# Layer 1's convolution and layer 2's embedding as parts of layer 2's table of slots

## The chip, the core and the metric

One core of a Trainium2 chip runs the whole program. Its engines take their instructions in order, each from its own queue: PE (TensorE, matrix products into PSUM), DVE (VectorE), ACT (ScalarE), POOL (GpSimd, which also issues the indirect gathers) and SP (which issues most DMAs). The metric is the device time of one execution in microseconds; ten runs of the kernel before give the median. All data are 32-bit floats.

## The reference, cut to what matters

Four images of 128 channels, 48x48, pass through a state-space layer (layer 0), a deformable convolution (layer 1), eight performer blocks (layer 2), a mixture of experts, causal attention (layer 3) and a second mixture. The change touches layers 1 and 2.

```python
# layer 1: deformable 3x3 convolution, batch norm, relu
off_out = conv3x3(x, w_off) + b_off             # 27 channels: dy, dx, mask for 9 taps
py, px = gy + ky + dy, gx + kx + dx             # where each tap samples
sampled = bilinear(x, py, px) * sigmoid(mask)   # 4 corners, zero outside
out = relu(scale * einsum('oik,bikhw->bohw', weight, sampled) + shift)
# layer 2, t = tokens of out: [4, 2304, 128]
h = layernorm(t) @ tok_W + tok_b + pe           # the embedding
for i in range(8):                              # performer
    h = h + attn(layer_norm(h), i)              # key features are summed over all tokens of an image
    h = h + gelu(layer_norm(h) @ W1[i] + b1[i]) @ W2[i] + b2[i]
    if i == 3: h = gelu(h @ enc + enc_b) @ dec + dec_b
t = t + tanh(h)
```

## The kernel before

An image has 2304 tokens: 18 tiles of 128 tokens, or 6 blocks of 384 (`BLK`, three tiles, `G3`). Four images make 24 blocks (`NBL`). The state of the tokens is one SBUF tile `T` (`h` in layer 2) of 128 partitions x 72 tiles x 128 channels.

**Layer 1 (`_layer1`, L878 to L970)** comes first and alone. For an image it loads the 27 offset channels (L908), works out positions, table rows and four corner weights per tap on DVE (L911 to L939, the mask's sigmoid on ACT at L934), and then goes through the 18 tiles. A tile has nine taps. For each tap POOL gathers 128 rows of 4x128 values from a table in DRAM that layer 0 wrote (L949; a row holds the four corners; eight buffers `g`), DVE multiplies by the four corner weights into another buffer `gw` (L956), and PE turns and sums the four corners at once as four ordinary products with the identity (L962), three taps to a PSUM tile `pt`. ACT copies `pt` to `sT` (L965). Then nine products with the convolution's weights and one with the shift (L968, L969) and a relu on ACT (L970) give the tile of `T`. The order is left to a scheduler.

**The embedding (L1108 to L1129)** follows, image by image: `T` is stored to DRAM as `kept` (L1115), its statistics are measured on DVE (`measure`, L1078 and L1079), `finish` raises the variance to -1/2 on POOL (L1086), the normed block (L1093) is turned on PE, copied, multiplied by `tok_w` (L1126), and added to the position table `pe` (L1127, which holds `tok_b` too since L1110).

**Layer 2's table of slots.** Its eight layers have 8 x 24 = 192 blocks, and a loop over slots writes the order of PE, ACT, DVE and POOL out by hand; SP's order alone is the scheduler's. In slot s the block s gets its keys and values (`k1`, `k2`, `k3`; `k0` of block s+1 norms on POOL and adds a bias to `h` on POOL, L1165), the block s-9 its queries (`q0` to `q2`; `LAG` = 9), the block before that its attention output (`q3` to `q6`), and the block s-12 its feed-forward part (`f0` to `f4`; `FLAG` = 12). `rotated` adds two halves of a rotary embedding on POOL (L1180). After an image's last keys, pieces put aside (`some`) sum its key features (L1301, L1311). So slots 0 to 8 have key work alone, slots 9 to 11 have queries too, and from slot 12 on all three.

Of the kernel before, what the change touches and what calls it, by code (L numbers as in the profile page):

```python
# [15 lines left out]
F32 = mybir.dt.float32  # L16
# [7 lines left out]
P = 128  # L24
NB = 4
# [845 lines left out]
def layer1(env, io, table, offs, T):  # L871


    with ExitStack() as ctx:
        _layer1(ctx, env, io, table, offs, T)


def _layer1(ctx, env, io, table, offs, T):  # L878
    nc, tc, ident = env.nc, env.tc, env.ident
    cp = ctx.enter_context(tc.tile_pool(name="l1c", bufs=1))  # L880
    sp = ctx.enter_context(tc.tile_pool(name="l1s", bufs=2))
    ps = ctx.enter_context(tc.tile_pool(name="l1p", bufs=3, space=PSUM))
    po = ctx.enter_context(tc.tile_pool(name="l1o", bufs=2, space=PSUM))
# [3 lines left out]
    w = cp.tile([P, TAPS, C], F32, name="w")  # L887
    nc.sync.dma_start(w, io["l1_w"])


    def row(name):
        t = cp.tile([P, C], F32, name=name)
        nc.scalar.dma_start(t, io[name].to_broadcast([P, C]))
        return t

    scale, shift, mean, var = (row("l1_" + n) for n in ("gamma", "beta", "mean", "var"))
    nc.vector.tensor_scalar_add(var, var, 1e-5)
    nc.scalar.sqrt(var, var)
    nc.vector.reciprocal(var, var)
    nc.vector.tensor_mul(scale, scale, var)  # L900
    nc.vector.tensor_mul(mean, mean, scale)
    nc.vector.tensor_sub(shift, shift, mean)
    for t in range(TAPS):
        nc.vector.tensor_mul(w[:, t, :], w[:, t, :], scale)

    for b in range(NB):
# [35 lines left out]
        for i in range(NT):  # L942
            sT = sp.tile([P, TAPS, P], F32, name="sT")
            for t0 in range(0, TAPS, 3):
                pt = ps.tile([P, 3, P], F32, name="pt")
                for t in range(t0, t0 + 3):
                    g = sp.tile([P, 4 * C], F32, name="g", bufs=8)
                    j = i * TAPS + t
                    nc.gpsimd.indirect_dma_start(  # L949
                        out=g,  # L950
                        out_offset=None,
                        in_=table,
                        in_offset=bass.IndirectOffsetOnAxis(ap=idx[:, j : j + 1], axis=0),
                    )
                    gw = sp.tile([P, 4, C], F32, name="gw", bufs=4)
                    nc.vector.tensor_mul(  # L956
                        gw,
                        g.rearrange("p (q c) -> p q c", c=C),
                        wq[:, i, t, :].unsqueeze(2).to_broadcast([P, 4, C]),
                    )  # L960
                    for q in range(4):
                        nc.tensor.matmul(  # L962
                            pt[:, t - t0, :], gw[:, q, :], ident, start=q == 0, stop=q == 3
                        )
                nc.scalar.copy(sT[:, t0 : t0 + 3, :], pt)  # L965
            out = po.tile([P, C], F32, name="out")
            for t in range(TAPS):
                nc.tensor.matmul(out, sT[:, t, :], w[:, t, :], start=t == 0, stop=False)  # L968
            nc.tensor.matmul(out, env.ones_row, shift[:1, :], start=False, stop=True)  # L969
            nc.scalar.activation(T[:, b * NT + i, :], out, AF.Relu)  # L970
# [25 lines left out]
def layer2(env, io, T):  # L996


    with ExitStack() as ctx:
        _layer2(ctx, env, io, T)  # L1000
# [5 lines left out]
FLAG = LAG + 3  # L1006

# [6 lines left out]
def _layer2(ctx, env, io, T):  # L1014
# [33 lines left out]
    tok_b = cp.tile([P, 1, C], F32, name="tok_b")  # L1048
# [25 lines left out]
    def measure(st, b, j):  # L1074
        mv, rstd = st
        s6 = sp.tile([P, G3, nc.vector.BN_STATS_DIM], F32, name="s6", bufs=3)
        for g in range(G3):
            nc.vector.bn_stats(out=s6[:, g, :], in_=h[:, b * NT + j * G3 + g, :])  # L1078
            nc.vector.bn_aggr(out=mv[:, j * G3 + g, :], in_=s6[:, g, :])  # L1079
# [8 lines left out]
    def normed(st, b, j, engine, name):  # L1088
        mv, rstd = st
        xn = sp.tile([P, G3, C], F32, name=name, bufs=1)  # L1090
        for g in range(G3):
            i = j * G3 + g
            engine.tensor_scalar(  # L1093
                xn[:, g, :],
                h[:, b * NT + i, :],
                mv[:, i, 0:1],
                rstd[:, i : i + 1],
                op0=ALU.subtract,
                op1=ALU.mult,
            )  # L1100
        return xn
# [5 lines left out]

    pe = bp.tile([P, NT, C], F32, name="dk")  # L1108
    nc.scalar.dma_start(pe, io["l2_pe"])
    nc.gpsimd.tensor_add(pe, pe, tok_b.to_broadcast([P, NT, C]))  # L1110
    st1 = []
    for b in range(NB):
        first = stats()
        for j in range(NBLK):
            nc.sync.dma_start(kept[:, at(b, j), :], h[:, at(b, j), :])  # L1115
            measure(first, b, j)
        finish(first, 0, NT)
        st1.append(stats())
        for j in range(NBLK):
            pt = psum(P, BLK)  # L1120
            transposed(normed(first, b, j, nc.vector, "fn"), pt)
            xT = sp.tile([P, BLK], F32, name="uT", bufs=1)
            nc.scalar.copy(xT, pt)
            pp = psum(P, G3, C)
            for g in range(G3):
                nc.tensor.matmul(pp[:, g, :], xT[:, bass.ts(g, P)], tok_w, start=True, stop=True)  # L1126
            nc.vector.tensor_add(h[:, at(b, j), :], pp, pe[:, j * G3 : (j + 1) * G3, :])  # L1127
            measure(st1[b], b, j)
        finish(st1[b], 0, NT)  # L1129
# [32 lines left out]

    def biased(w, r, b, j):
        hb = h[:, at(b, j), :]
        nc.gpsimd.tensor_add(hb, hb, w["bias"][:, r : r + 1, :].to_broadcast([P, G3, C]))  # L1165

    def rotated(w, name, b0, b1, xT, j):

        a = bass.ts(j, BLK)
        pa, pb = psum(P, BLK), psum(P, BLK)  # L1170
        nc.tensor.matmul(pa, w[name], xT, start=True, stop=True)  # L1171
        nc.tensor.matmul(pb, w[name + "r"], xT, start=True, stop=True)  # L1172
        q = sp.tile([P, BLK], F32, name=name, bufs=1)
        r = sp.tile([P, BLK], F32, name="r")
        sq = sp.tile([P, BLK], F32, name=name + "sq", bufs=1)
        nc.vector.scalar_tensor_tensor(q, pa, b0, cos[:, a], op0=ALU.add, op1=ALU.mult)

        nc.scalar.activation(sq, pa, AF.Square, bias=b0)
        nc.vector.scalar_tensor_tensor(r, pb, b1, sin[:, a], op0=ALU.add, op1=ALU.mult)
        nc.gpsimd.tensor_add(q, q, r)  # L1180
        return q, sq
# [19 lines left out]
    def k0(y, n):  # L1201
        t, s, b, j = block(y, n)
        t["xn"] = normed(y.first[b], b, j, nc.gpsimd, "kn")
        biased(y.w, 0, b, j)

    def k1(y, n):
# [10 lines left out]
        t["xT"] = sp.tile([P, BLK], F32, name="xT", bufs=LAG + 2)  # L1217
# [45 lines left out]
    def largest_keys(s):  # L1263
# [7 lines left out]
        def tokens():  # L1271
# [4 lines left out]
            s["xb"] = sp.tile([P, P], F32, name="xb")  # L1276
# [225 lines left out]
    with tc.manual_schedule(engines=ORDERED):  # L1502
        for slot in range(-1, NL * NBL + FLAG + 3):
            i, n = divmod(slot, NBL)
            if i + 1 < NL and n == FLAG + 4:
                layers[i + 1] = Layer(i + 1, layers[i].after)
            if i + 1 < NL and n == NBL - 3:
                prepare(layers[i + 1].w)
            do(q0, slot - LAG)
            do(f1, slot - FLAG)  # L1510
            do(m0, slot - FLAG - 2)
            do(k1, slot)
            some(1)
            do(q3, slot - LAG - 1)
            do(f3, slot - FLAG - 1)
            do(k2, slot)
            do(f2, slot - FLAG)
            do(m1, slot - FLAG - 2)
            some(1)
            do(q1, slot - LAG)  # L1520
            do(k0, slot + 1)
            do(q4, slot - LAG - 1)
            some(1)
            do(k3, slot)
            do(whole, slot)
            do(f0, slot - FLAG + 1)
            do(q5, slot - LAG - 1)
            some(1)
            do(q2, slot - LAG)
            some(1)  # L1530
            do(m2, slot - FLAG - 2)
            do(q6, slot - LAG - 1)
            do(f4, slot - FLAG - 1)
            do(m3, slot - FLAG - 2)

# [656 lines left out]
def program(tc, io, out):  # L2192
    with ExitStack() as ctx:
        env = Env(ctx, tc)
        nc = tc.nc
        with ExitStack() as conv:
            dr = conv.enter_context(tc.tile_pool(name="dr", bufs=1, space=DRAM))
            table = dr.tile([NB * TROWS, 4 * C], F32, name="table")
            offs = dr.tile([P, NB * NT, NOFF], F32, name="offs")
            layer0(env, dr, io, table, offs)  # L2200
            state = ctx.enter_context(tc.tile_pool(name="state", bufs=1))
            T = state.tile([P, NB * NT, C], F32, name="T")
            layer1(env, io, table, offs, T)
        layer2(env, io, T)
# [140 lines left out]
```

## Time and profile before

| what | us |
|---|---|
| median of 10 runs (lowest, highest) | 12663.49 (12636.17, 12673.59) |
| the profiled execution's own time | 12670.15 |
| its span | 12668.0 |
| layer 1's first gather (L949) starts | 5415.3 |
| layer 1's last gather starts | 6318.2 |
| first key copy of layer 2's slot 0 (L1218) starts | 6454.5 |

Times in the profile count from the start of the span. Layer 0 fills the time up to about 5400, layer 2's slots that from 6454 to about 10716, and the rest belongs to the mixtures and layer 3. In rows of groups, the numbers behind the bar are the group's busy time, the mean of one in ns, and the idle time of the engine in front of them with what ended it. PE's records count two per product of 32-bit floats, and one per turn in transpose mode; matmuls are pipelined, so the busy time of a group is less than count times mean. In tables by window the columns are busy us and number of records of each engine, the granted clock of PE as a share of full speed, the busy share of the DMA engines, and GB/s.

### The profile page before, as it was taken

The numbers are of one execution on the slowest core, as the hardware profiler recorded it, in microseconds if no ns is written. First come the engines' busy times: TensorE is split into PE (matmuls) and PEld (weight loads), VectorE is DVE, ScalarE is ACT, GpSimd is POOL, SyncE is SP. The second block draws the span as 40 slices with busy tenths as digits, with TensorE's granted clock in tenths as the row PEclk, the third lists the DMA queues.
The fourth block names the chain that finished last, engine by engine and source line by source line (L and its number), as shares of the span: only waits on it lengthen the run. The fifth ranks groups of instructions, "written<-read, shape, count | busy, mean of one in ns | idle before, by whom it ended". The sixth has DMA issues, their size and how long they took to land.

```text
span 12668.0 us, 192717 instructions
## 1 busy us (share of the span) xinstructions
PE 10962.5 (87%) x71150; PEld 8366.5 (66%) x71150; DVE 8504.5 (67%) x15484; ACT 6888.1 (54%) x13189; POOL 4428.9 (35%) x4775
## 2 busy tenths in 40 slices
PE   6878778877887787689879999999999997799997
PEld 4667666766676666478857777877777776433333
DVE  3998889888888889555456566566565655344444
ACT  3777767777777777411135556555565555232222
POOL 1443333333333334277733333333333332000001
PEclk9999999999999999799979999999999998799998
DMA  2221222122212222266600000000000001200003
GB/s 104 67 70 65 77 79 69 65 75 83 68 65 74 84 65 67 66 180 195 194 13 2 4 4 3 4 2 4 3 3 4 1 1 43 84 6 6 8 8 125
DMA packets 307846, 677.50 MB, mean 53 GB/s; under 512 B 39108, under 2 KB 128984, under 8 KB 304864
## 3 DMA queue, kind: packets, MB, share of 16 engines
q1 hardware_dynamic: 254032, 493.49, 11.8%
q0 software_dynamic: 51840, 169.91, 4.6%
q8 instruction: 571, 9.36, 0.3%
q14 instruction: 363, 2.97, 0.1%
q10 hardware_dynamic: 1040, 1.77, 0.0%
HBM read 602.63 MB, written 71.85 MB: 53 GB/s over the span
## 4 chain that ended last, share of the span: by engine, by line
PE 39%; DVE 6%; ACT 3%; POOL 2%; issue 2%; DMA 2%; SPq 0%; DVEq 0%; ACTq 0%; POOLq 0%
PE psum L1425 4%; PE psum L1417 4%; PE pc L1311 3%; PE psum L1361 3%; PE scT L2061 3%; PE sc L2007 3%; PE out L2090 3%; PE psum L1331 2%; PE psum L1171 2%; POOL g L949 2%; PE psum L1172 2%; DMA g<-table,idx 2%; PE psum L1105 2%; PE psum L1249 1%; PE psum L1350 1%
## 5 line engine op out<-in xcount | busy, mean ns | idle before, releaser
L565 ACT ACTIVATE hs<-ps,bct 128x256 f32<-128x256 f32 x4608 | 1853.4, 474 | 1174.6 <-PE ps L559 1123.0
L559 PE MATMUL ps<-ident,h 128*128 128x128 f32 x9216 | 1489.4, 293 | 781.4 <-DVE h L545 609.2
L559 PEld LDWEIGHTS ps<-ident,h 128*128 128x128 f32 x9216 | 1077.2, 148 | 1166.1 <-DVE h L545 716.3
L573 PE MATMUL yp<-ident,hs 128*128 128x128 f32 x9216 | 1404.7, 288 | 28.4 <-ACT ys L588 28.4
L505 ACT ACTIVATE dA<-delta,l_Al 128x768 f32<-128x768 f32 x1536 | 1388.2, 936 | 0.3
L512 POOL TENSOR_TENSOR h<-du,rB 128x512 f32<-128x512 f32 x768 | 1077.2, 1403 | 766.2 <-PE ps L559 690.4
L573 PEld LDWEIGHTS yp<-ident,hs 128*128 128x128 f32 x9216 | 1156.9, 150 | 84.0 <-ACT ys L588 57.6
L545 DVE TENSOR_TENSOR_SCAN h<-dA,h 128x256 f32<-128x256 f32 (+1 forms) x1024 | 1084.8, 1059 | 27.2
L545 DVE TENSOR_TENSOR_SCAN h<-dA,carry,h 128x768 f32<-128x768 f32 x512 | 1024.1, 2000 | 10.6 <-ACT dA L505 10.6
L1165 POOL TENSOR_TENSOR T<-T,bias 128x384 f32<-128x384 f32 x384 | 383.7, 999 | 1560.4 <-DVE fn L1093 1520.2
L487 POOL TENSOR_SCALAR_AFFINE_SELECT dB<-bct 128x512 f32<-128x512 f32 x768 | 743.6, 968 | 385.6 <-PE b L519 246.8
L2069 ACT ACTIVATE pT<-scT 128x768 f32<-128x768 f32 (+2 forms) x504 | 377.6, 749 | 894.3 <-PE scT L2061 894.0
L519 PE MATMUL b<-dB,duT 128*128 128x128 f32 x6144 | 828.5, 279 | 0.8 <-ACT duT L445 0.8
L545 DVE TENSOR_TENSOR_SCAN h<-dA,carry,b 128x512 f32<-128x512 f32 x512 | 646.1, 1262 | 269.5 <-PE b L519 249.8
L949 POOL DMA_INDIRECT g<-table,idx x648 | 703.5, 1086 | 264.0 <-issue 151.0
L519 PEld LDWEIGHTS b<-dB,duT 128*128 128x128 f32 x6144 | 769.0, 197 | 2.4 <-POOL h L512 1.2
L962 PE MATMUL pt<-ident,gw 128*128 128x128 f32 x5184 | 661.4, 283 | 96.8 <-DVE gw L956 93.4
L956 DVE TENSOR_TENSOR gw<-g,wq 128x512 f32<-128x512 f32 x648 | 446.1, 693 | 421.0 <-DMA g<-table,idx 351.8
L552 POOL COPY carry<-h 128x2 f32<-128x2 f32 x512 | 97.3, 190 | 1781.5 <-DVE h L545 1723.7
L962 PEld LDWEIGHTS pt<-ident,gw 128*128 128x128 f32 x5184 | 608.7, 193 | 144.4 <-DVE gw L956 111.1
L2017 DVE TENSOR_REDUCE mx<-sc 128x2 f32<-128x1024 f32 (+3 forms) x400 | 428.4, 1071 | 363.9 <-PE sc L2007 358.8
L516 DVE TENSOR_TENSOR h<-du,rB 128x512 f32<-128x512 f32 x768 | 632.3, 823 | 3.5 <-DMA rB<-rows 3.5
(345 smaller groups left out, 22968.2 us busy)
## 6 DMA issues: line engine op xcount, KB each, us to landing
rB<-rows SPq DMA_DIRECT2D x768, 384.0 KB, 3.4
w<-f_w SPq DMA_DIRECT2D x64, 1024.0 KB, 12.2
table<-y SPq DMA_DIRECT2D x9, 2304.0 KB, 17.6
table<-tok SPq DMA_DIRECT2D x16, 1152.0 KB, 10.1
g<-table,idx POOLq DMA_INDIRECT x648, 3.7
xb<-x SPq DMA_DIRECT2D x48, 192.0 KB, 2.8
xn<-xn SPq DMA_DIRECT2D x48, 192.0 KB, 3.4
yd<-y SPq DMA_DIRECT2D x4, 2304.0 KB
```

Of the source, the lines that this page charges most:

```text
L487: nc.gpsimd.affine_select(out=x.dB[n], in_=x.bc[:, m0 : m0 + CT // P, n : n + 1].to_broadcast([P, CT // P, P]), pattern=[[0, CT // P], [1, ...
L505: nc.scalar.activation(dA, x.delta[:, d, :], AF.Exp, scale=A[:, d, x.k, n : n + 1])
L512: nc.gpsimd.tensor_mul(h[:, 1, own], x.du[:, 1, own], x.rB[n][:, own])
L516: nc.vector.tensor_mul(x.h[n][:, :, own], x.du[:, :, own], b)
L519: nc.tensor.matmul(b0[:, bass.ts(m, P)], x.duT[:, m, :], x.dB[n][:, m, :], start=True, stop=True,)
L545: nc.vector.tensor_tensor_scan(h, da, b, initial=first, op0=ALU.mult, op1=ALU.add)
L559: nc.tensor.transpose(tt[:, m, bass.ts(d, P)], x.h[n][:, d, bass.ts(2 * q + m, P)], ident)
L565: nc.scalar.activation(hs, tt[:, m, :], AF.Copy, scale=x.bc[:, 2 * q + m, NS + n : NS + n + 1])
L573: nc.tensor.matmul(yp[:, q, (2 * d + m) * P : (2 * d + m + 1) * P], hs[:, bass.ts(d, P)], ident, is_transpose=True, start=n == 0 and m == ...
L949: nc.gpsimd.indirect_dma_start(out=g, out_offset=None, in_=table, in_offset=bass.IndirectOffsetOnAxis(ap=idx[:, j : j + 1], axis=0),)
L962: nc.tensor.matmul(pt[:, t - t0, :], gw[:, q, :], ident, start=q == 0, stop=q == 3)
L1417: nc.tensor.matmul(pg, y.w["w1"][:, bass.ts(f, P)], t["uT"], start=True, stop=True)
```

## The change: positions in front, the convolution three slots ahead, the embedding two

- **Positions.** A new function `positions_of` does L908 to L939 for all four images and stores table rows and corner weights to two DRAM tensors, `index` and `corners`. Each block later loads its own part (27 columns of rows, 27x4 weights) through SP.
- **The convolution** of block n is written into slot n-3. Its steps are nine turns (three taps each), three outputs, and `done` (store to `kept`, statistics, POOL's power). The loop begins three slots earlier. In a turn DVE multiplies in place, for the first of three taps it also adds two pairs of corners; PE turns 2+4+4 tiles in transpose mode and sums them in PSUM; ACT copies. After a turn, `fetch` issues further gathers on POOL: up to 10 ahead in blocks 0 to 15 (six buffers `g` and four places in `T` that belong to image 3's tiles), up to 6 ahead in blocks 16 to 23. A gather into a buffer waits for PE's turns of what was in it.
- **The embedding** of block n is written into slot n-2 as three steps (norm on ACT, turn, project). It loads its part of the position table, which is stored to DRAM once with `tok_b` added.
- The steps (16 in a full slot: turns, outputs, norm, turn, project) are dealt out over 17 places of a slot (`one`).
- **While gathers go on** (to slot 20), three works of layer 2 leave POOL: the norm of `k0` goes to ACT, the bias adds and the rotary add to DVE (`spare`).
- Smaller ones: the convolution's weights lie in layer 2's weight buffers; the next layer's weights are named at slot 22 in place of 16 and prepared at 22 in place of 21; `xT` has 9 buffers in place of 11, `xb` one in place of two.

```diff
-        for i in range(NT):
-            sT = sp.tile([P, TAPS, P], F32, name="sT")
...
+        a = slice(b * NT, (b + 1) * NT)
+        nc.sync.dma_start(index[:, a, :], idx.rearrange("p (t k) -> p t k", k=TAPS))
+        nc.sync.dma_start(corners[:, a, :, :], wq)
...
+AHEAD = 3
+HOLES = 17
+NG = 6
+NGT = 4
+NGTAPS = 16 * G3 * TAPS
...
+        def gather(self, k):
+            own = (self.n * G3 * TAPS + k) % (NG + NGT) - NG
+            if own >= 0 and self.n * G3 * TAPS + k < NGTAPS:
+                own = (NB - 1) * NT + own * 4
+                g = h[:, own : own + 4, :].rearrange("p q c -> p (q c)")
+            else:
+                g = sp.tile([P, 4 * C], F32, name="g", bufs=NG)
+            self.g[k] = g
+            nc.gpsimd.indirect_dma_start(
...
+        def corners(self, k):
+            g = self.g[k].rearrange("p (q c) -> p q c", c=C)
+            nc.vector.tensor_mul(g, g, self.wq[:, k, :].unsqueeze(2).to_broadcast([P, 4, C]))
+            if k % 3:
+                return 4
+            nc.vector.tensor_add(g[:, :2, :], g[:, :2, :], g[:, 2:, :])
+            return 2
...
+        def turn(self, k0):
+            parts = {}
+            for k in range(k0, k0 + 3):
+                parts[k] = self.corners(k)
+            pt = psum(P, 3, P)
+            for k in range(k0, k0 + 3):
+                g = self.g.pop(k)
+                for q in range(parts[k]):
+                    nc.tensor.matmul(pt[:, k - k0, :], g[:, bass.ts(q, C)], ident, is_transpose=True,
...
+            nc.scalar.copy(sT, pt)
...
+    def fetch(done):
+        nonlocal fetched
+        while fetched < min(done + NG + (NGT if done < NGTAPS else 0), NBL * G3 * TAPS):
+            n, k = divmod(fetched, G3 * TAPS)
+            if n not in sampled:
+                sampled[n] = Sampled(n)
+            sampled[n].gather(k)
+            fetched += 1
...
+    def spare():
+        return nc.vector if gathering else nc.gpsimd
...
-        for slot in range(-1, NL * NBL + FLAG + 3):
+        fetch(0)
+        for slot in range(-AHEAD, NL * NBL + FLAG + 3):
...
+            early = convolve(slot + AHEAD)
+            steps = embed(slot + AHEAD - 1)
+            for place, step in zip((8, 10, 15), steps):
+                early.insert(place, step)
...
+            def one():
+                nonlocal passed
+                passed += 1
+                while early and (total - len(early)) * HOLES < total * passed:
+                    early.pop(0)()
+
             do(q0, slot - LAG)
+            one()
             do(f1, slot - FLAG)
             do(m0, slot - FLAG - 2)
+            one()
             do(k1, slot)
             some(1)
+            one()
...
```

## The prediction

> **What bounds the kernel now.** I read the table by window first, to see which engine fills each stage.
>
> ```profile
> core 0: us, PE busy (x) PEld busy (x) DVE busy (x) ACT busy (x) POOL busy (x), PEclk, DMA share, GB/s
> 5415.00:6327.00 912.00, 831.25 (x6627) 774.80 (x6627) 467.52 (x741) 123.60 (x289) 707.20 (x653) 0.99 0.66 192
> 6327.00:6454.00 127.00, 60.22 (x221) 45.55 (x220) 71.32 (x353) 11.76 (x25) 28.12 (x12) 0.51 0.14 51
> 6454.00:6780.00 326.00, 303.84 (x1796) 236.81 (x1795) 181.06 (x534) 173.35 (x358) 134.31 (x151) 0.98 0.00 1
> 7300.00:7820.00 520.00, 510.92 (x3195) 412.19 (x3195) 316.21 (x999) 304.74 (x593) 193.16 (x219) 0.99 0.01 3
> ```
>
> The rows are the convolution, the embedding, slots 0 to 20 (the key copy L1218 has 42 records there, two per slot), and 24 slots of the steady state. The steady state is PE's: 510.9 of 520 us, 21.7 us a slot, with DVE at 13.2 us, ACT 12.7 and POOL 8.0. In the convolution PE looks full too, but the groups of that window and POOL's timeline say otherwise.
>
> ```profile
> L949 POOL DMA_INDIRECT g<-table,idx x648 | 703.5, 1086 | 264.0 <-issue 151.0 <-ACT m L934 66.8 <-DMA g<-table,idx 24.4
> L962 PE MATMUL pt<-ident,gw 128*128 128x128 f32 x5184 | 661.4, 283 | 96.8 <-DVE gw L956 93.4
> L956 DVE TENSOR_TENSOR gw<-g,wq 128x512 f32<-128x512 f32 x648 | 446.1, 693 | 421.0 <-DMA g<-table,idx 351.8 <-PE pt L962 61.1 <-PE out L969 5.6
> L968 PE MATMUL out<-w,sT 128*128 128x128 f32 x1296 | 156.5, 275 | 0.0
> L969 PE MATMUL out<-l_beta,ones_row 1*128 1x128 f32 x144 | 34.8, 321 | 0.0
> ```
>
> ```profile
> 5430.72 1.16 POOL L949 DMA_INDIRECT g<-table,idx  x1 [0.30 <-issue]
> 5432.18 1.00 POOL L949 DMA_INDIRECT g<-table,idx  x1 [0.30 <-issue]
> 5433.49 1.16 POOL L949 DMA_INDIRECT g<-table,idx  x1 [0.30 <-issue]
> 5434.96 1.10 POOL L949 DMA_INDIRECT g<-table,idx  x1 [0.30 <-issue]
> ```
>
> POOL issues gathers back to back, 0.30 us between two, and waits for buffers hardly at all (24.4 us for earlier gathers, against 151 of plain issue). First to last gather is 5415.3 to 6318.2, so one costs 902.9 / 647 = 1.395 us. Layer 1 is bound by POOL; PE is close behind (831 of 912). DVE waits for gathers that land (351.8 us).
>
> **The change, step by step.** What decides is when slot 21 begins, the first without gathers: from there on work is as before, and before it begins at 6780. I sum by engine for one block.
>
> *POOL.* 27 gathers x 1.395 = 37.7 us. The change cannot shorten that, only put other engines' work beside it. To it come powers in POOL's queue, for `done` and for the embedding:
>
> ```profile
> L1086 POOL TENSOR_TENSOR rstd<-rstd,half 128x3 f32<-128x3 f32 x48 | 40.7, 861 | 24.0 <-DVE rstd L1085 24.0
> L1350 PE MATMUL psum<-ident,e 128*128 128x128 f32 x216 | 29.3, 275 | 3.0 <-DVE kmax L1251 3.0
> ```
>
> 0.86 + 0.30 between = 1.16 us each: 40.0 us a block; from slot 10 `q6` adds one (41.2), from 13 `f4` another (42.3). The norm, bias and rotary adds that leave POOL (8.0 a slot without powers 6.3) are not in it.
>
> *DVE.* 27 multiplications x 0.693 = 18.7; nine adds of 128x256, between a 128x128 one (0.29) and a 128x384 one (0.55), taken 0.42: 3.8; statistics, six pairs of 0.272 + 0.182, plus small ones 0.7: 3.4; the embedding's add 0.556. Sum 26.5 us. A full slot has 13.2 of its own and four adds from POOL at 0.55: 2.2. So 41.9 in slots 12 to 20, some 31 in key-only slots.
>
> *PE.* 90 turns in one pass in place of 216 records: the nearest row is the transposes L1350, 29.3 / 216 = 0.136, so 12.2; output 54 records x 156.5/1296 = 6.5, shift 6 x 0.242 = 1.5, embedding 2.1. Sum 22.3 against 35.5 before. With 21.3 of a full slot: 43.6. Key-only slots: about 6.5 + 22.3 = 29. ACT: nine copies of 0.478, three relus, six norms of 0.28, one copy: 7.3 + 12.7 = 20, no bound.
>
> So key-only slots are POOL's with room, and full slots have POOL, PE and DVE within 2 us of each other: nothing is cover for anything there.
>
> *Stalls.* A gather lands 3.7 us after its issue, so 2.3 after its end. With ten buffers, the last tap of a turn has 7 gathers (9.8 us) behind it before POOL runs out; landing 2.3, DVE 0.7, PE 0.5 to 1.2 take about 4.5, so 5 us are spare for queues. But between the ninth turn and the next slot's first, POOL passes the powers, which wait for output, relu and statistics: PE 2.7 + relu 0.3 + DVE 2.3, then the first turn's 2.5 on DVE and 1.3 on PE, 9 us and more, against about 6 buffers x 1.395 = 8.4 still free. I take 2.5 us lost in key-only slots (0 to 6), 5 where query work stands between. In blocks 16 to 23 (slots 13 to 20) six buffers hold two turns. From PE's end of one turn to that of the next but one: three gathers to landing 2 x 1.395 + 3.7 = 6.5, then 1.5 on DVE and PE: 8 us for two turns, 36 a slot, less than POOL's 42 but with no room; each wait of PE or DVE behind slot work adds. Bounds 44 (PE's sum) and 60 (2 us more a turn); I take 50, nearer to the sum since before those engines had idle time only behind PE.
>
> *Start.* Before, DVE began positions at 5409 and the first gather went out at 5415, images 1 to 3 being hidden behind gathers. Now the first block's rows go through DRAM, their load stands in SP's queue behind the store of the fourth image's rows, and POOL's add for `pe` (5.04 us at L1110) is in front of the first gather. Four images at 6.5 us of DVE (L911 to L939) = 26, store and load 2 x 3 (kept stores land in 3.0): 5409 + 26 + 6 = 5441, taken 5445. Bounds 5435 and 5460: SP also carries 26 more weight loads of 0.33 us in layer 0's end, where its queue is empty for 10 us at a time, and the big tables load here (the one for sin took 10.6).
>
> *Sum.* Slots -3 to 8: 12 x 42.5 = 510. Slots 9 to 12: 4 x 46 = 184. Slots 13 to 20: 8 x 50 = 400. 5445 + 1094 + 2 for the last embedding in slot 21 = 6541, against 6780: 239 us less. What is gained is the embedding's 127 and most of slots 0 to 20's 326; what is paid is 44 us of start, powers, stalls and three engines at their limit. Smaller edits cost nothing: weights load when buffers come free (SP waits for semaphores, at slots 8 to 13 before), `xT`'s ninth buffer is read on PE ahead of its overwriting, SP's block loads have a block's time of lead. Without that cover a late load costs about 3 us a block, 72 in all.
>
> 12668.0 - 239 = 12429 for the span. The median of the runs is 4.5 below the profiled span: **12425**.
>
> **Two prices that the sum leaves out.** The granted clock was 0.51 in the embedding at 47% PE busy, 0.98 in slots 0 to 20 at 93%. Key-only slots will have 29 of 42.5, 68%, which no row matches; I take full clock, and the third case below is the other end. The Trainium skill ("TensorE: Matmul & The Clock Gate", Part 4: PE-mode transpose) speaks against me: transposes don't count as PE work for the gate, over half of the new block's PE time is such turns, and by it these slots would run at half clock.
>
> Gathers took from 0.942 us, mean 1.086, while DVE multiplied for 446 of 912 us, 49%. In the new slots DVE is in instructions with two SBUF inputs for (18.7 + 3.8 + 2.2) / 46 = 54%; if the 0.144 above the shortest goes with that share, a gather costs 0.015 more, 10 us in all. The rule that makes me ask is the skill's "GPSIMD Engine Reference", 1. Specifications: GpSimd contends with DVE instructions that have two SBUF inputs.
>
> **The rivals.**
> - *POOL's floor.* All stalls hide: 24 x 40.0 + 21 powers x 1.16 = 984; 5445 + 984 = 6429, -351, 12313. For it: POOL hardly waited for buffers before. Against: full slots ask 43.6 of PE.
> - *Half clock* in the 12 key-only slots: at 0.51, as in the embedding, PE's 29 become 57; 57 for 42.5 is +174, 12599. For it: that row, of short bursts like these. Against: PE would then be busy all the time, and stretches above 80% had 0.9 or more.
> - *Slower.* The landing is exposed in every turn: PE's turns stand behind slot work that waits for DVE, which stands behind multiplications that wait for gathers, so POOL gets buffers back only after the chain. 9 x 2.3 = 21 us on top of 41 a slot: 24 x 62 = 1488, 6933, +153, 12816. It decides from (6780 - 5445) / 24 = 55.6 us a slot, 1.6 of 2.3 us exposed. For it: every order here is written out by hand and no engine may pass a wait. Against: ten buffers give 5 us of room in 16 of 24 blocks.
>
> **Chances.** Forecast 0.60 (its own range 12350 to 12510), POOL's floor 0.16, half clock 0.14, slower 0.07, a tie between 0.03. The range takes in the first three nearly whole: 12300 to 12610. About 0.2%, 25 us, is what a measurement of this kernel can tell from no change: faster 0.90, same 0.03, slower 0.07.
>
> **What would show it.** Gathers still 1.35 to 1.45 us apart within a slot and a pause of POOL once a slot, behind powers; slots of 40 to 45 us up to slot 8 and about 50 from slot 13; first gather near 5445; the key copy of slot 21 near 6540; steady slots at 21.7. PE's clock below 0.8 before slot 9 says half clock; POOL waiting on PE before most gathers says the slower case; a later slot that is longer than before would be a cost that I left out.

## The result, and the profile after

The changed kernel takes 12726.9 us (median; 12702.0 to 12739.3) where the kernel before takes 12660.7 in the same runs: a ratio of 1.0052, interval 1.0043 to 1.0061. The forecast was 12425, with a range that ended at 12610. So the kernel became slower by 66 us where 239 less were forecast.

The table by window of the changed kernel shows the stages: blocks alone in front of layer 2's keys, slots 0 to 7, slots 9 to 12, slots 13 to 20, and 24 slots of the steady state. Its columns are as before: busy us and records of each engine, then PE's granted clock, the DMA share and GB/s.

```profile
core 0: us, PE busy (x) PEld busy (x) DVE busy (x) ACT busy (x) POOL busy (x), PEclk, DMA share, GB/s
5435.00:5569.00 134.00, 93.34 (x491) 76.25 (x492) 83.25 (x175) 20.77 (x50) 105.84 (x99) 0.70 0.67 199
5569.00:5935.00 366.00, 251.15 (x1479) 209.68 (x1477) 224.80 (x507) 95.23 (x226) 247.34 (x233) 0.86 0.57 166
6000.00:6234.00 234.00, 165.13 (x933) 135.78 (x932) 143.71 (x344) 67.42 (x149) 117.18 (x115) 0.83 0.43 125
6234.00:6825.00 591.00, 421.54 (x2430) 350.35 (x2429) 309.76 (x781) 173.42 (x354) 248.26 (x241) 0.85 0.34 101
6826.00:7346.00 520.00, 509.36 (x3186) 410.45 (x3184) 317.16 (x1005) 306.04 (x597) 194.39 (x221) 1.00 0.01 4
```

In slots 13 to 20 a slot takes 591 / 8 = 74 us, and no engine is full: PE 71%, DVE 52%, POOL 42%, ACT 29%. The steady state is what it was (21.7 us a slot). The forecast's stages against the trace, by the key copies (`xT`):

| stage | forecast | changed kernel |
|---|---|---|
| first gather | 5445 | 5435.3 |
| slots -3 to 8 | 510 | 564.8 |
| slots 9 to 12 | 184 | 234.5 |
| slots 13 to 20 | 400 | 591.4 |
| slot 21 begins | 6541 | 6826.0 |
| from there to the end of the span | 5888 | 5893.7 |

Two thirds of the 285 us by which slot 21 is late arise in slots 13 to 20. (Slot 8 alone, between the second and the third line of the table, took 65.0 us, which no run explains.) The view of waits for these slots (who waited for what: us in total, times, longest) says who holds whom.

```profile
PE psum L1170 <- issue: 151.3, 41, 5.5
POOL g L1145 <- PE psum L1170: 150.1, 52, 17.6
...
DVE kv L1455 <- PE pc L1448: 55.2, 6, 10.4
...
DVE mx L1471 <- PE psum L1468: 44.1, 8, 7.8
DVE T L1569 <- PE psum L1562: 36.2, 9, 4.4
...
DVE kmax L1388 <- ACT dk L1387: 32.2, 8, 4.4
...
DVE T L1529 <- PE psum L1526: 29.2, 8, 5.0
...
DVE rd L1507 <- PE psum L1498: 25.4, 8, 4.5
...
DVE g L1155 <- DMA g<-table,idx: 10.8, 10, 2.8
```

PE's waits of any size stand ahead of the turns (L1170): its 421.5 us of work and 169.5 us of waiting there fill the stage. DVE stands still for layer 2's results from PE and ACT, and for gathers only 10.8 us in eight slots: rows have landed long before their multiplication is due. POOL waits for PE's turns; with rows that land so early, this is an effect. "issue" on PE's line hides the cause, which the timeline shows. First DVE, then PE, in slot 15:

```profile
6405.48 0.56 DVE L1569 TENSOR_TENSOR T<-T,psum 128x384 f32<-128x384 f32 x1 [4.40 <-PE psum L1562]
6406.06 0.29 DVE L1038 BATCH_NORM_STATS2 s<-T 128x6 f32<-128x128 f32 x1
...
6407.28 0.66 DVE L1155 TENSOR_TENSOR g<-g,wq 128x512 f32<-128x512 f32 x1
6407.97 0.43 DVE L1158 TENSOR_TENSOR g<-g 128x256 f32<-128x256 f32 x1
```

```profile
6402.49 2.94 PE L1562 MATMUL psum<-w,gl 128*128 128x128 f32 x24
6408.50 4.22 PE L1170 MATMUL psum<-ident,g 128*128 128x128 f32 x20 [3.06 <-issue]
```

DVE waits 4.40 us for PE's feed-forward product (L1562), adds it, measures, and only then comes to the turn's multiplication and add, which end at 6408.40. PE, which has the turn next in its order, waits 3.06 us for them and begins at 6408.50. Then DVE will wait for PE again. The two work by turns. (That DVE is what "issue" hides was read from the timeline here; the run e10 below names it.)

### The profile page after: what moved, and what is told of

It reads as the page before. It is cut to its first block, busy times and chain, and to the rows that moved or that the text cites. A ratio compares the mean times of both kernels' runs of the same rounds, so it can differ in the third digit from the quotient of the medians.

```text
span 12719.7 us, 187316 instructions
## 1 busy us (share of the span) xinstructions
PE 10757.6 (85%) x68126; PEld 8131.8 (64%) x68126; DVE 8599.0 (68%) x15779; ACT 6958.3 (55%) x13327; POOL 4318.7 (34%) x4691
## 4 chain that ended last, share of the span: by engine, by line
PE 57%; DVE 23%; ACT 11%; issue 6%; DMA 2%; POOL 1%; SPq 0%; ACTq 0%; DVEq 0%; POOLq 0%
DVE h L545 8%; ACT hs L565 5%; PE psum L1562 4%; PE ps L559 4%; PE psum L1554 4%; PE pc L1448 3%; PE psum L1498 3%; PE pf L187 3%; PE scT L2233 3%; PE yp L573 3%; PE sc L2179 3%; PE out L2262 3%; DVE h L516 2%; PE psum L1170 2%; PE b L519 2%
## 5 line engine op out<-in xcount | busy, mean ns | idle before, releaser
L573 PEld LDWEIGHTS yp<-ident,hs 128*128 128x128 f32 x9216 | 1157.4, 151 | 81.8 <-ACT ys L588 57.7
L1301 POOL TENSOR_TENSOR T<-T,bias 128x384 f32<-128x384 f32 x352 | 351.8, 999 | 1458.5 <-DVE fn L1069 1442.4
L1145 POOL DMA_INDIRECT g<-table,idx x476 | 501.4, 1053 | 437.6 <-PE psum L1170 214.8
L1170 PE MATMUL psum<-ident,g 128*128 128x128 f32 x1588 | 330.4, 361 | 341.3 <-issue 222.3
L1388 DVE TENSOR_REDUCE kmax<-psum 128x8 f32<-128x352 f32 x576 | 275.6, 520 | 437.5 <-ACT dk L1387 430.9
L1562 PE MATMUL psum<-w,gl 128*128 128x128 f32 x4608 | 547.0, 275 | 1.8 <-ACT wqsq L1314 1.5
```

The lines of the kernel that those rows point to most:

```text
L573: nc.tensor.matmul(yp[:, q, (2 * d + m) * P : (2 * d + m + 1) * P], hs[:, bass.ts(d, P)], ident, is_transpose=True, start=n == 0 and m == ...
L1170: nc.tensor.matmul(pt[:, k - k0, :], g[:, bass.ts(q, C)], ident, is_transpose=True, start=q == 0 and k == k0, stop=q + 1 == parts[k] and k ...
L1562: nc.tensor.matmul(pp[:, g, :], t["gl"][:, f, bass.ts(g, P)], y.w["w2"][:, f, :], start=f == 0, stop=f == DFF // P - 1,)
```

## The experiments

Theories at the start: (a) lock-step: a turn's multiplications stand in the order directly ahead of its turns on PE, so DVE and PE wait for each other; (b) the ring of six gather buffers in the last blocks; (c) the adds that went to DVE, with the bias add's wait for the norm that went to ACT (47.6 us of DVE's waits in slots 0 to 7); (d) PE's clock of 0.85.

These ran on other chips than the runs above, where the kernel before itself takes about 12,765 us; so ratios are compared, and the changed kernel was run there again. Times by stage are from key copies in each trace; in the last column stand PE's busy share and granted clock in slots 13 to 20.

| run | ratio to before | slots 0-7 | 9-12 | 13-20 | PE in 13-20 |
|---|---|---|---|---|---|
| changed kernel again (r_after) | 1.0002 [0.9992, 1.0013] | 409 | 250 | 591 | 71%, 0.85 |
| e2_six | 12801.5 us, one time | 425 | 250 | 584 | |
| e3_mul_ahead | 0.9842 [0.9826, 0.9858] | 370 | 209 | 490 | 82%, 0.85 |
| e4_bias_later | 12748.8 us, one time | 390 | 237 | 580 | |
| e5_ring | 0.9822 [0.9806, 0.9839] | 352 | 200 | 466 | 83%, 0.89 |
| e6_pool_adds | 0.9945 [0.9926, 0.9965] | 365 | 231 | 576 | |
| e7_both | 0.9812 [0.9794, 0.9831] | 358 | 210 | 449 | 84%, 0.90 |
| e8_filler | 0.9819 [0.9800, 0.9839] | 378 | 210 | 456 | 92%, 0.96 |
| e9_act | 0.9813 [0.9797, 0.9830] | 367 | 204 | 450 | 84%, 0.90 |
| e10_filler_after | 1.0034 [1.0023, 1.0046] | 422 | 243 | 595 | 78%, 0.90 |
| e11_ring_after | 0.9996 [0.9987, 1.0006] | 406 | 242 | 584 | 72%, 0.84 |

In the first row the trace is of the slowest of ten times (12796 against a median of 12774). Slots 0 to 7 differ from chip to chip, 366 us in the first trace of the changed kernel and 409 in this one, so small differences in that column carry little; slots 13 to 20 took 591 us in both.

**The two kernels on one other chip.**

> The kernel before, unchanged, for a trace beside that of the changed kernel on one chip: in the last runs the kernel before took 12,760 us, 100 more than in the runs shown, while the variants' gathers and steady slots had the durations of the changed kernel's trace. If the gathers' stage is what differs from chip to chip, the 648 gathers take 1.395 us each where the time is near 12,660, and about 1.55 where it is near 12,760; slots 0 to 20 take 326 us in either case.

> The changed kernel, unchanged, on the same chip as the others of this call. If chips differ only where POOL's gathers set the pace, this one stays at 12,727 within 25 us whatever the kernel before takes, since its gathers do not set the pace; if chips differ as a whole, it is 0.5% above the kernel before here too.

The kernel before took 12772.1 in its profiled run, the changed one 12773.9 (median of ten, 12737 to 12796). The first expectation was half right: the convolution's blocks start 42.0 us apart in place of 37.7, and slots 0 to 20 take 328; but a gather's own duration is no longer (mean 1009 ns against 1086). The second missed: the changed kernel took 47 us more too. The table by window of the kernel before there, in the convolution:

```profile
5800.00:6000.00 200.00, 171.65 (x1347) 163.50 (x1346) 86.19 (x136) 24.84 (x58) 130.70 (x131) 0.95 0.62 177
```

On the first chip its clock was 0.99 in that stage. On this one DVE waited 403 us for PE's turns (L962), against 60 on the first, and POOL 186 us for DVE's `gw`, against 19: here PE holds the chain, where POOL did. That the lower clock is the reason is likely, but not shown. So the ratio of the two kernels depends on the chip, between no difference and 0.5% slower; none of this explains the missing 239 us.

**The convolution alone, whole (e1).**

```diff
-AHEAD = 3
+AHEAD = 24
```

> AHEAD goes from 3 to 24: the whole convolution runs in slots -24 to -1, alone but for its own norm and statistics, and only the embedding stays in slots -2 to 21. Every theory of the loss that needs layer 2's work beside the turns (lock-step of DVE and PE, ring of six buffers, bias waiting for the norm) expects blocks as in slots -3 to -1 of the changed kernel, 37 to 40 us each (mean 38.7): 5435 + 24 x 38.7 = 6365 for the first key copy, against 6454 before; slots 0 to 20 take 326 us as before, so slot 21 starts near 6691 (before 6780, changed kernel 6826). Total about 12,590 us, within 12,560 to 12,620. If the convolution alone in this form is slower than in slots -3 to -1 (six buffers in the last 8 blocks matter: +2 us each), 12,610.

12709.4 us, ratio 0.9958 [0.9941, 0.9974]: faster than before, by 50 us, but the expectation missed. First key copy at 6504.6, not 6365: only the first two blocks take 38.7 us, and the later ones 43.9 on average. Slots 0 to 20 then took 323 us, about as in the kernel before (326). The table by window for the stage:

```profile
5520.00:6490.00 970.00, 654.45 (x3492) 534.84 (x3491) 545.37 (x1145) 148.42 (x356) 676.07 (x637) 0.73 0.58 171
```

No engine is above 70%, and there are no layer 2 products here: a block in this form takes 43.9 - 27 x 1.395 = 6 us more than its gathers by itself: 2.3 for the two powers, which the forecast had counted, and 3.0 in which POOL waits for the statistics ahead of a power (67 us in all).

**Fewer buffers (e2), more buffers (e11).** In e2 the four places in `T` are not used, so that all blocks have six buffers. In e11 they are used for longer, as rows of image 3 are still free (all four to block 17, then as many as `LATE` says); its core:

```diff
-NGTAPS = 16 * G3 * TAPS
+LATE = {NBL - 6: 3, NBL - 5: 3, NBL - 4: 2, NBL - 3: 1}
```

> Six gather buffers in all 24 blocks in place of ten in the first 16. Ring theory (slots 13 to 20 are long, at 68 to 89 us, because six buffers hold two turns only): slots -3 to 12 lengthen towards those, key-only slots from 46 to 60 and more, slots 9 to 12 from 58 to 70; +200 us or more, 12,900 or more. Lock-step theory (PE and DVE wait for each other in written order and gathers have long landed): slots 13 to 20 as they are, key-only slots at most 2 to 4 us longer, total within 12,727 to 12,780.

> The changed kernel with more gather buffers in the last blocks alone (ten in blocks 16 and 17, nine in 18 and 19, eight in 20, seven in 21, in place of six). Ring theory: slots 13 to 18 are 8 to 15 us shorter each, 50 to 90 in all, a ratio of 0.993 to 0.996 to the kernel before. Lock-step theory: gathers have landed long before their multiplication is due (12 us after their issue in the median, 3.7 where DVE waits for them), so no slot changes by more than 2 us: 0.998 to 1.002.

With six buffers everywhere slots 0 to 7 take 53 us each against 51, less than the difference between chips, and later slots no more than before; the ring theory asked for 60 and more, and for 12,900 us. More buffers in blocks 16 to 21 gave 0.9996 against 1.0002. Theory (b) fell, from both sides, though e2 rests on one time, which is also above the 12,780 that the lock-step theory allowed.

**Multiplications a step ahead (e3).** A turn's multiplications are split off and written after the previous turn; nothing else moves.

```diff
-        def turn(self, k0):
-            parts = {}
+        def multiply(self, k0):
             for k in range(k0, k0 + 3):
-                parts[k] = self.corners(k)
+                self.parts[k] = self.corners(k)
+
+        def turn(self, k0):
+            parts = self.parts
...
             sampled[n].turn(k)
+            multiply(n * G3 * TAPS + k + 3)
             fetch(n * G3 * TAPS + k + 3)
```

> The three multiplications of a turn move one step ahead of its transposes in the written order, so PE finds them done. Lock-step theory: about 2.2 us less at each of nine turns, 20 us off each of slots 13 to 20 (160), 10 off each of slots 9 to 12 (40), 2 to 5 off key-only slots: 200 us less or more, about 12,520 us (12,470 to 12,600), and DVE's waits ahead of the turns on PE fall from 170 us in slots 13 to 20 to under 60. Ring theory: no change in slots 13 to 20, since a buffer is freed by PE's turn as late as before; 12,727 within 20.

Ratio 0.9842 against 1.0002: 1.6%, 204 us less, with the same instructions. By the traces slots 13 to 20 lost 102 us, slots 9 to 12 41, slots 0 to 7 40 (less sure, as said), slot 8 16. Of waits in slots 13 to 20 the view shows:

```profile
PE psum L1172 <- DVE g L1159: 60.4, 18, 4.7
...
DVE g L1156 <- DMA g<-table,idx: 41.5, 40, 3.1
...
DVE T L1577 <- PE psum L1570: 31.3, 8, 4.4
...
DVE mx L1479 <- PE psum L1476: 21.9, 8, 3.2
...
DVE kv L1463 <- PE pc L1456: 14.2, 6, 4.1
```

PE's idle time ahead of the turns fell from 169.5 us to 87.4 (I expected under 60), and with it DVE's waits for PE fell, which nobody moved: `kv` from 55.2 to 14.2, `mx` from 44.0 to 21.9 (both as on the first chip in r_after's trace). That is what one expects of a lock-step when one side is loosened. Only now does DVE meet gathers that have just landed (41.5 against 10.8).

**The bias add later (e4), and norm and adds back on POOL (e6).** In e4 the bias add becomes a step of its own behind the key block's other work:

```diff
         t["xn"] = normed(y.first[b], b, j, engine, "kn")
+
+    def k0b(y, n):
+        t, s, b, j = block(y, n)
         biased(y.w, 0, b, j)
...
             do(k3, slot)
...
+            do(k0b, slot + 1)
```

In e6 one part of the change is undone:

```diff
-        return nc.vector if gathering else nc.gpsimd
+        return nc.gpsimd
...
-        engine = nc.scalar if gathering else nc.gpsimd
+        engine = nc.gpsimd
```

> The key step's bias add (on DVE, waiting for the norm on ACT that reads the same rows) is written after the key block's other work. If this wait is what fills key-only slots: 4 to 6 us off each of slots 0 to 12, 50 to 70 in all, 12,665 us, and DVE's wait at the bias add, 47.6 us in slots 0 to 7, is gone. If the same time is lost behind the next instruction instead: 12,727 within 15.

> One part of the change undone: norm, bias add and rotary adds of layer 2 stay on POOL while gathers run, as they were. If the bias add's wait on DVE (47.6 us in slots 0 to 7) and DVE's four adds a slot cost time: key-only slots 4 to 6 us shorter, slots 13 to 20 2 to 5 shorter, 60 to 100 us less, near 12,640. If POOL is what then holds the gathers (its 8 us a slot stand in front of them, and each waits for DVE): key-only slots 52 and more, +80 us or more, 12,810. My estimate is between: POOL has room in full slots (41% busy) but not in key-only ones (68%); +20.

e4's one time, 12748.8, lies among the ten of the unchanged kernel (12737 to 12796): no gain shown. Its trace says why: the wait of the bias add for the norm (68.8 us in slots 0 to 7 of r_after) is gone, but DVE's wait for ACT's `dk` at `kmax` grew from 28.9 to 59.8: much of the time is lost at another instruction, as the second branch of the expectation had it. e6 is below all ten (12690 and 12697), 80 us less than their median. My own estimate for it, +20, was wrong. Its table by window, slots 0 to 7:

```profile
5569.00:5934.00 365.00, 262.48 (x1476) 212.00 (x1474) 225.76 (x482) 85.25 (x202) 286.01 (x276) 0.84 0.58 168
```

POOL is busy 286 us there against 245 in the changed kernel, and the stage is not longer for it (365 against 409 here and 366 on the first chip). Which of the three works matters (norm, bias add, rotary add) is not told apart.

**Both, and what is left (e5, e7, e8, e9).** e5 is e3 with e11's buffers, e7 is e5 with e6's edit. e8 adds eight transposes of the identity ahead of each turn, which the turn overwrites; e10 does so in the changed kernel. In e9 ACT multiplies the third tap of each turn.

```diff
             pt = psum(P, 3, P)
+            for r in range(8):
+                nc.tensor.matmul(pt[:, 0, :], ident, ident, is_transpose=True, start=r == 0, stop=r == 7)
```

```diff
+            if k % 3 == 2:
+                for q in range(4):
+                    nc.scalar.activation(g[:, q, :], g[:, q, :], AF.Copy, scale=self.wq[:, k, q : q + 1])
+                return 4
             nc.vector.tensor_mul(g, g, self.wq[:, k, :].unsqueeze(2).to_broadcast([P, 4, C]))
```

> The multiplications a step ahead (as in the run before), and with it more buffers in the last blocks: ten in blocks 16 and 17, nine in 18 and 19, eight in 20, seven in 21, where six were. If the ring is the next limit once the lock-step is loosened (a multiplication a step ahead holds three buffers for longer): 5 to 8 us less in each of slots 13 to 18, 30 to 45 us in all, near 12,525. If only the order of DVE and PE is: within 15 us of 12,565.

> The two parts that each helped, together: multiplications a step ahead with more buffers in the last blocks (241 us below the changed kernel on one chip), and norm, bias add and rotary adds of layer 2 left on POOL (80 below it). If they heal different waits (order of DVE and PE; DVE's adds and the bias add's wait for the norm): key-only slots stay at POOL's 44 and gain nothing, slots 9 to 20 lose another 2 to 3 us each, 30 to 40 in all, near 12,495. If both only relieve the same lateness of DVE: no more than 10 us below 12,533. If POOL, now 8 us a slot busier, becomes the bound of key-only slots, which stand at 44 in both: those go to 46 or more and the sum is 12,530 to 12,560.

> As e7_both, with eight more transposes of the identity in front of each turn, overwritten by the turn: 8 x 0.136 = 1.1 us of PE at full clock, 10 us a block, in time in which PE waits for DVE or for a slot's chain. If the clock follows how much PE is kept busy (0.75 with 64% busy, 0.85 with 72%, 0.89 with 83%, 0.98 with 93%): it rises to 0.95 and more in slots 0 to 20, PE's other work shrinks by up to a tenth (3 us in key-only slots, 5 in full ones), and the time is within 20 us of e7_both or below it. If the clock does not answer: the fillers cost PE 10 us a block where PE is near its limit, slots 13 to 20 are 5 to 10 us longer each, +60 us or more.

> As e7_both, with the third tap of each turn multiplied on ACT, four activations of 128x128 at about 0.28 us, in place of one DVE instruction of 0.69: DVE 6.2 us a block less, ACT 10 more (it is busy 35% in slots 13 to 20). If DVE's lateness is still what PE waits for: 3 to 5 us off each of slots 9 to 20, 40 to 60 less than e7_both. If PE at its clock sets the pace by now, or ACT's copies are held up behind the multiplications: within 15 us of it, or slower by up to 60.

> The changed kernel with eight transposes of the identity in front of each turn, overwritten by it; they stand where PE waits for the turn's multiplications on DVE, so they fill that wait (2 to 2.5 us a turn against 8 x 0.136 = 1.1). If PE's granted clock is part of the loss (0.85 in slots 13 to 20 with PE 72% busy): it rises to 0.95 or more there, PE's 53 us a slot without the fillers fall to 46 to 48, and as PE's work is on the chain from PE to DVE and back, slots 13 to 20 are 4 to 7 us shorter, key-only slots 1 to 3: 50 to 80 us below the changed kernel, a ratio of 0.994 to 0.996 to the kernel before. If PE's speed is hidden behind DVE's lateness: within 20 us of the changed kernel, 0.9987 to 1.002.

e5, e7, e8 and e9 lie between 0.981 and 0.982, and their intervals overlap; e5's lead on e3 is within the intervals too. They are about 1.8% below both kernels. So e6's 80 us do not come on top of the mended order (e7 0.9812, e5 0.9822): both edits seem to relieve the same lateness of DVE. Fillers raised the clock. The tables by window, slots 13 to 20, of e7, e8 and e10:

```profile
6196.00:6645.00 449.00, 377.52 (x2435) 317.81 (x2434) 302.58 (x740) 160.29 (x331) 297.95 (x292) 0.90 0.44 130
```

```profile
6234.00:6690.00 456.00, 417.63 (x2994) 364.06 (x2994) 303.75 (x741) 160.00 (x331) 297.57 (x292) 0.96 0.43 128
```

```profile
6322.00:6917.00 595.00, 464.39 (x2994) 393.40 (x2993) 309.49 (x781) 174.69 (x356) 251.11 (x242) 0.90 0.35 100
```

From e7 to e8 PE has some 560 records more, 76 us at 0.136, but is busy only 40 more: the rest of its work got quicker, and the time did not. In the changed kernel (e10) the clock rose from 0.85 to 0.90 only, and the slots took 595 us, against 591: with a clock of 0.95 I expected 4 to 7 us less a slot. In all it is 0.3% slower than the changed kernel, outside both branches of the expectation. The fillers took 81.8 us there; PE's waits ahead of the turns fell by 39 (169.3 to 130.6), and its other work by 39 (421.7 to 382.6). So theory (d) found no support, but it is not ruled out for a small part: fillers that stood in no wait can have hidden a gain of up to those 39 us, 5 of the 24 by which a slot is over the forecast. With fillers ahead of them, the turns' waits also get their name:

```profile
PE psum L1174 <- DVE g L1158: 113.6, 41, 4.6
```

L1158 is DVE's add in the turn's own step. Taking 6.2 us a block off DVE, for 10 more on ACT (e9), gave nothing either. What holds the best variants at 56 us a slot in slots 13 to 20 is open; other places for the 16 steps within a slot were not tried.

## Why the prediction was wrong, step by step

- **Start** (5445): 5435.3, at the lower bound. Right in its reasons; ten us in favour.
- **POOL's floor** (37.7 us a block, 40.0 with powers): not refuted, since no block went below it for long. Gathers took 1.057 us on average against 1.086 before, where the sentence on contention had 0.015 more each. Its premise failed, not its sign: since the slots were longer, DVE was in instructions with two SBUF inputs for 40% of 5435 to 6826 (553 us at L1155, L1158, L1301 and L1316), not 54%, against 49% before. Stage by stage the mean falls with that share, from 1.079 at 55% (slots -3 to -1) to 1.045 at 31% (slots 13 to 20), which fits contention but does not prove it. Some 10 us hung on it. The floor counts 21 further powers where slots 10 to 20 and 13 to 20 have 19; that is 2 us.
- **Key-only slots** (42.5): 45.7 in slots 0 to 7 on the first chip. The pause behind the powers that I foresaw is there; its size, 2.5 beside the 40.0, is too small even with no layer 2 beside it (43.9 - 40.0 = 3.9 in e1). Slot 8, which the forecast counts among them, took 65.0.
- **Sums of PE and DVE** (43.6 and 41.9 a full slot): DVE was 309.76 / 8 = 38.7, near enough. PE was 421.54 / 8 = 52.7, a fifth more, at a mean clock of 0.85 and not 1. Of the 9.1 us more, 6.6 are the turns (150.7 / 8 = 18.8, priced at 12.2), the records that follow a wait. Where fillers made PE's other work quicker (e10, e8), the time did not fall.
- **Stalls: the step that failed.** "I take 50, nearer to the sum since before those engines had idle time only behind PE", and 46 in slots 9 to 12. Measured: 74, above even my upper bound of 60, and 59. I worked out the stall as a matter of the ring: landing, multiplication, turn, with so many buffers. The ring was not it (e2, e11), and landing was hidden. (It comes 2.6 us after a gather's end, not 2.3: I had taken the 1.395 between two starts for the gather's 1.09.) What I left out is that DVE serves PE within the same step of an order that no engine may leave. In the kernel before, the multiplications went to separate buffers `gw` and a scheduler let DVE run ahead of PE; in the change the turn's three multiplications, up to 2.5 us, stand behind whatever DVE waits for, and PE's order has nothing to do before the turn. Adding busy times of engines comes near the time only if each has work in hand while another is late. e3 restores one step of lead and with it 204 us; its slots 13 to 20 still take 61 us each, and what makes up the rest is open.
- **"The norm, bias and rotary adds that leave POOL" as a small sum on DVE** (2.2 a slot): leaving them on POOL is worth 80 us (e6). I priced their busy time alone. That it is their place in the orders of DVE and ACT that costs is my reading: e4 moved one of them on DVE and showed no gain.
- **Rivals.** The slower one had the right sign and the right sentence, "no engine may pass a wait", but the wrong mechanism, an exposed landing in every turn; its mark, POOL waiting for PE before most gathers, showed in part (150.1 us, 52 waits for 209 gathers) as an effect of the lock-step. Half clock: its mark, below 0.8 before slot 9, showed in slots -3 to -1 alone (0.70); slots 0 to 7 had 0.86, well above 0.51.
- **The rest of the span** (5888): 5894.

With the order mended and e7's other two edits the forecast's size comes back: e7's 0.9812 is about the forecast's 12425 / 12663.5 = 0.9812. But that is chance for the most part: the kernel before is slower by 119 us on that chip (12779.6), and slots 13 to 20 still take 449 us where 400 were forecast.

## What to carry to other kernels

Where an order is written out by hand, an engine that prepares another's operand should do so at least one step ahead; a sum of busy times comes near the time only when each engine has such a lead. Look in the trace for two engines that each wait for the other, at different lines, with nothing full, and try the order first: here it gave 204 us, more buffers and fillers for the clock gave none, and work taken off DVE gave 80 before the order was mended and nothing after. When moving work off a busy engine, ask what stands behind it in its new queue, not only how much it weighs.

## What the runs showed of the hardware

- PE's granted clock is recorded as 1.00 or 0.50, with nothing between, in every trace here; the 0.70 to 0.96 of the tables are means over stretches. Cut into windows of 2 us, the changed kernel's slot 15 has 1.00 up to 6408, 0.65 to 6410, 0.50 to 6412 and then 1.00 again, behind PE's wait that ended at 6408.50.
- The mean rose when fillers raised PE's busy share: 0.85 to 0.90 from 71% to 78% (e10), 0.90 to 0.96 from 84% to 92% (e8). The fillers are transposes and nothing else, so they did count, and in e8 they took 276 ns in the mean, as the transposes of the steady state do (275). The Trainium skill ("TensorE: Matmul & The Clock Gate", Part 4: PE-mode transpose) says that the full clock "doesn't engage" for transpose mode, which "doesn't count as PE-busy the same way"; the runs here disagree.
- The share alone doesn't give the mean clock: 82% with 0.85 in e3, 78% with 0.90 in e10.
- Chips differ by about 0.8% in the kernel before (12,661 against 12,766) with the same instructions. The difference arises in the convolution, at a clock of 0.93 to 0.95 in place of 0.98 to 1.00; the steady slots agree (510.9 us of PE in 520 on both).
